# One-hot gathers on TensorE: the picks and sums of two units side by side, twice as many groups gathered wholly by TensorE, and the comparisons dealt out anew between VectorE and ScalarE

## The chip, the cores and the metric

The kernel runs on one core of a Trainium2 chip. A core has five engines that run at the same time, each through its own queue in order: TensorE (PE in the profile; its weight loads, PEld, are listed apart), VectorE (DVE), ScalarE (ACT), GpSimd (POOL) and SyncE (SP, which here only issues transfers). They wait for each other by semaphores. The metric is the device time of one execution in microseconds (us). The times before are the median of three runs; the profile is of one further execution.

## The reference

One layer of a graph network over 6250 nodes with 64 features and 206,250 edges, which are sorted by the node they point to (`dst`):

```python
h = jnp.maximum(_layernorm(x, axis=-1), 0.0)
msg = relu(h[src] + edge_attr)                      # one row per edge
agg = segment_sum(msg, dst, num_segments=6250)
x = x + relu((h + agg) @ W1 + b1) @ W2 + b2
```

The costly part is `h[src]`, a gather of 206,250 rows of 64 numbers, and the sum of the messages by `dst`.

## The kernel before

**Groups.** The edges are cut into 269 groups of 768: 128 partitions by 6 columns. The first five groups are a prologue, in which the layer norm is also made. For each later group GpSimd gathers three of the six columns, row by row, with indirect transfers (`gather`, L204, buffer `xg`), nine groups ahead. The other three columns are gathered by TensorE, as products with one-hot matrices. Three columns so treated are a *unit*. In 12 *whole* groups (`WHOLE`) TensorE gathers all six columns, and GpSimd none: such a group is two units. There are 276 units in 138 *sets* of two, and 46 *chunks* of three sets.

**How a row is picked.** A node's row of `h` lies in SBUF as three bf16 parts that add up to float32 (`hp`, 3x64 columns). The picking has two steps. In the first, the *slots*, `found` (a one-hot matrix: which node of 128 is wanted in each of 32 slots) multiplies `hp`: `slots_of`, L497, in column tiles of 128x32, 52 matmuls a unit. The result goes from PSUM (`half`, three banks in turn) to `picked` by a ScalarE copy (`slots_out`, L506). In the second step, the *picks*, `backs` (a one-hot matrix from slots to edges) multiplies `picked`: `pick`, L513, 18 matmuls of 128x128 weights a unit, 192 columns each. They add onto a PSUM bank that ScalarE has filled with the edge attributes (`room`, L522; two banks in turn). VectorE adds up the three parts (`messages`, L600), after it has added the gathered columns (L597), and ScalarE applies the relu (L602, `msg`).

**The one-hot matrices** are comparisons. `found` of a set has two blocks of 1536 columns and one of 256, for the last nodes (`find`, L465); all three are made by VectorE. `backs` of a set has six blocks of 768 columns: VectorE makes five (`back`, L484), and ScalarE the last in two passes, |a-b| and then relu(1-|a-b|) (`back_far` L474, `back_near` L477). What they compare against are lists of slots, broadcast to all partitions by SyncE's transfers (`source_load`, `spot_load`), one of each a set. The lists come from the *rank work* of a chunk: VectorE, TensorE and ScalarE find which slot each edge takes (`rank_at` to `source`, L280 to L347), about two chunks ahead; on TensorE these are the count (L285, L287), a transpose (L325) and the source matmuls (L339), all through one PSUM bank, `rows`.

**The sums.** For each unit a one-hot matrix of 32 nodes (`oh`, L581, two buffers) multiplies the messages: `window_sum`, L612, float32, column tiles of 128x64, 12 matmuls for six columns and 6 for three. The result lies in a corner of the first `half` bank. VectorE adds it to `z` two units later (`sum_into_z`, L575) at a column that it holds in a register; the columns of 16 groups are loaded into registers at a time (`window_start`, L442).

**Row blocks.** When all edges of 512 nodes are summed, the two dense layers follow: `hidden` (L631, TensorE, then ScalarE L634), `result` (L642, then L644) and `store` (VectorE L650 and L651, then a transfer), one step at each call of `blocks_behind`. There are 12 such blocks in the loop; `rows` serves them too.

**The order** is written out by hand, in `half(u)`, one call for each unit: what is called first is first in its engine's queue. For unit u of set k, TensorE gets: the sums of u-1, the slots of half of set k+1, the picks of u+1, the rank work if any. VectorE gets, in an even half: `messages(u)`, the one-hot of u, `backs` 3 and 4 of set k+1, z of u-2, row blocks, the first and the last block of `found` of set k+2. In an odd half: `messages(u)`, the one-hot, the second block of `found`, z of u-2, row blocks, `backs` 0 to 2 of set k+2. The rank work comes last in a half. The `beats` pace GpSimd's gathers: a gather waits for the TensorE instruction that its beat names.

Of the kernel before, what the change touches and what calls it, by code (L numbers as in the profile page):

```python
# [9 lines left out]
F32 = mybir.dt.float32  # L10
I32 = mybir.dt.int32
I16 = mybir.dt.int16
BF16 = mybir.dt.bfloat16
# [31 lines left out]
H = 3  # L45
# [13 lines left out]
F0 = 5  # L59
SETS = 3  # L60
RG = 2 * SETS
HEAD, PERIOD = 2 * RG - 1, 4 * RG - 1
assert (NG + 1 - F0 - HEAD) % PERIOD == 0
# [18 lines left out]
def kernel(  # L82
# [163 lines left out]

    def stretches(t_sb, c0, c1):

        n, g0 = (HEAD, F0) if c0 == 0 else (PERIOD, F0 + HEAD + (c0 - 2) // 4 * PERIOD)
# [201 lines left out]
    def source_load(k):  # L451
        sources[k] = rank.tile([P, PARTS * 2 * S], I16, name="sources")
        nc.sync.dma_start(out=sources[k][:PP], in_=lines[k // SETS][k % SETS].rearrange("(o m) s -> o (m s)", o=1)
                          .to_broadcast([PP, PARTS * 2 * S]))

    def spot_load(k):
        spots[k] = rank.tile([P, 2 * H * P], BF16, name="spots")
        nc.sync.dma_start(out=spots[k], in_=spot_rows[k * 2 * H:(k + 1) * 2 * H, :]
                          .rearrange("(o t) s -> o (t s)", o=1).to_broadcast([P, 2 * H * P]))

    def find(k, b):
# [3 lines left out]
        nc.vector.tensor_scalar(found[k][:, b * PARTS:b * PARTS + n].rearrange("p m i s -> p (m i s)"),  # L465
                                sources[k][:, :n * 2 * S], nodes_of[:, b:b + 1], None, op0=ALU.is_equal)

    far = const.tile([P, 1], F32, name="far")
    nc.vector.tensor_scalar_mul(far, ids[:, Q - 1:], -1.0)
    dists = {}  # L470

    def back_far(k):
        dists[k] = rank.tile([P, 2 * H * P], BF16, name="dist", bufs=1)
        nc.scalar.activation(dists[k], spots[k].bitcast(I16), AF.Abs, bias=far)  # L474

    def back_near(k):
        nc.scalar.activation(backs[k][:, Q - 1].rearrange("p t s -> p (t s)"), dists.pop(k), AF.Relu,  # L477
                             bias=ones[:, 0:1], scale=-1.0)

    def back(k, q0, q1):  # L480
        if q0 == 0:
            backs[k] = hot.tile([P, Q, 2 * H, P], BF16, name="backs")
        for q in range(q0, min(q1, Q - 1)):
            nc.vector.tensor_scalar(backs[k][:, q].rearrange("p t s -> p (t s)"), spots[k].bitcast(I16),  # L484
                                    ids[:, q:q + 1], None, op0=ALU.is_equal)
        if q1 == Q:
            spots.pop(k)
# [17 lines left out]
    def slots_out(k, n0):  # L505
        nc.scalar.copy(picked[k][:, n0:n0 + 2], halves.pop((k, n0)))  # L506
# [66 lines left out]
    def sum_into_z(u):  # L573
        at = window_start(group_of(u))
        nc.vector.tensor_tensor(z[:, ds(at, W)], z[:, ds(at, W)], aggs.pop(u), ALU.add)  # L575
# [96 lines left out]
    def is_set(k):  # L672
        return 0 <= k < KS

    def half(u):
        g = group_of(u)
        k, i = divmod(u, 2)
        first = ((0, 2), (6, 8))[i]
        later = ((4,), (10,))[i]
        now = is_set(k + 1)  # L680
        if is_first(u):
            enter(g + AHEAD, beats[-G + H:])
        if i == 0:
            if is_set(k + 3):
                source_load(k + 3)
        elif is_set(k + 3):
            spot_load(k + 3)
        window_sum(u - 1)
        if u + 1 < U:
            room(u + 1)  # L690
        if now:
            for n0 in first:
                begun = slots_of(k + 1, n0)
                slots_out(k + 1, n0)
                if n0 == first[0]:
                    beats.append(begun)
            for n0 in later:
                beats.append(slots_of(k + 1, n0))
        if u + 1 < U:
            beats.append(pick(u + 1, range(H)))  # L700
        messages(u)
        if now:
            for n0 in later:
                slots_out(k + 1, n0)
        one_hot(u)
        if i == 0:
# [17 lines left out]
        chunk(u + 13, rank_count)  # L724
        chunk(u + 12, rank_of)
        chunk(u + 11, rank_marks)
        chunk(u + 11, rank_turn)
        chunk(u + 10, rank_holds)
        chunk(u + 10, rank_fits)
        chunk(u + 9, source)  # L730
        if g in CHECKS and is_first(u):
            find_left(CHECKS.index(g))

# [59 lines left out]
    for g in range(F0):  # L793
        for i in range(g * LOOK // F0, (g + 1) * LOOK // F0):
            tails_begin(i)
        messages(g - F0)
        one_hot(g - F0)
        if g == 0:
            rank_at(1)
            rank_count(1)  # L800
        if g == 1:
            rank_of(1)
            rank_marks(1)
            rank_turn(1)
        if g == 2:
            rank_holds(1)
            rank_fits(1)
            source(1)
        if g == 3:
            rank_at(2)  # L810
            rank_count(2)
        if g >= 1:
# [10 lines left out]

    for b in range(BB + 1):
        find(0, b)
    back_far(0)
    back(0, 0, Q)
    back_near(0)
    for n0 in range(0, 2 * Q, 2):
        begun = slots_of(0, n0)  # L830
        slots_out(0, n0)
# [5 lines left out]
    beats.append(pick(0, range(H)))  # L837
    for b in range(BB + 1):
        find(1, b)
    back_far(1)  # L840
    back(1, 0, 3)
    for u in range(U):
        half(u)
# [84 lines left out]
```

## Time and profile before

| | |
|---|---|
| median of three runs | 1082.63 us (1082.12 to 1085.3) |
| the profiled execution | 1080.78 us, span 1079.1 us |
| TensorE's granted clock over the span | 0.974 of full |
| picks, L513 | 4968 matmuls |
| slots, L497 | 14352 matmuls |
| sums, L612 | 3224 matmuls |
| `backs` on VectorE, L484 | 690, busy 255.8 us |
| `found`, L465 | 414, busy 206.1 us |
| adding up the parts, L600 | 276, mean 749 ns |
| ScalarE's two passes for `backs`, L474 and L477 | 138 each, means 952 and 954 ns |
| ScalarE's copies to `picked`, L506 | 828, mean 480 ns |
| GpSimd's gathers, L204 | 754, mean 1007 ns |

In the profile's timeline a line has the start in us, the time from the first start to the last end in us, the engine, the line of the kernel, the operation, output and inputs with their shapes, and how many instructions were put together. In brackets stands how long the engine had been idle before it, and which instruction ended that. Starts on TensorE are measured; its matmuls overlap, so a start-to-start distance says more than a duration. VectorE's and ScalarE's instructions also overlap by some 0.08 us where they follow each other without a wait. In the answer for one line, "DVEq" is VectorE's sequencer; the three numbers are the least, the median and the greatest duration in ns. In the windows of the span the columns are the window, its length, the busy time of TensorE, its weight loads, VectorE, ScalarE and GpSimd with the number of instructions, the granted clock, the share of the DMA engines and GB/s.

### The profile page before, as it was taken

To read this page: it belongs to the slowest core of one execution; us is meant where nothing else is said; L and a number is where in the kernel's file an instruction comes from. 1 tells how busy PE (TensorE), PEld (TensorE's weight loads), DVE (VectorE), ACT (ScalarE), POOL (GpSimd) and SP (SyncE) were. 2 spreads that over 40 slices of the span, in tenths; PEclk is the share of its full clock that TensorE was granted. 3 is DMA by queue.
4 is the path that set the end of the run, shared out by engine and by line. 5 is a ranking of instruction groups with operands and counts; after the bars stand their busy time and mean duration, and the time that the engine had idled before them with its cause. 6 is when DMAs were issued, how large, how long until landed. Compare 5 with 4: busy or idle time off the path is not lost.

```text
span 1079.1 us, 55140 instructions
## 1 busy us (share of the span) xinstructions
PE 994.9 (92%) x23185; PEld 865.5 (80%) x23185; DVE 960.5 (89%) x2686; ACT 940.6 (87%) x1979; POOL 793.9 (74%) x798
## 2 busy tenths in 40 slices
PE   3159999999999999999999999999999999999997
PEld 2148888888878888888888888888888888888885
DVE  8869889898998998998999898998999898998984
ACT  6459889899989998898998998998998998998985
POOL 7677777777777777777777777777777777777740
PEclk9659999999999999999999999999999999999998
DMA  6445566565655665665665656565656665655650
GB/s 207 126 117 150 164 164 187 141 178 158 188 143 150 180 190 143 170 169 165 163 174 149 184 157 165 155 199 156 161 148 187 164 170 154 185 158 161 167 132 10
DMA packets 115098, 172.36 MB, mean 160 GB/s; under 512 B 28444, under 2 KB 83613, under 8 KB 114845
## 3 DMA queue, kind: packets, MB, share of 16 engines
q1 hardware_dynamic: 89752, 143.03, 43.7%
q0 software_dynamic: 25088, 25.74, 13.5%
q8 instruction: 184, 3.01, 1.1%
q14 instruction: 70, 0.57, 0.2%
q10 hardware_dynamic: 4, 0.01, 0.0%
HBM read 164.85 MB, written 3.84 MB: 156 GB/s over the span
## 4 chain that ended last, share of the span: by engine, by line
PE 76%; DVE 10%; issue 5%; DMA 4%; ACT 3%; POOL 1%; DVEq 1%; SPq 0%; ACTq 0%
PE pick L513 34%; PE half L497 26%; PE half L612 10%; DVE backs L484 2%; DVE found L465 2%; DVE ea L600 2%; DMA xg<-h_rows,src_sb 2%; PE rows L339 2%; PE rows L642 1%; PE rows L631 1%; PE rows L287 1%; POOL xr L204 1%; DMA x<-in_x_dram 1%; DVE oh L581 1%; PE rows L285 1%
## 5 line engine op out<-in xcount | busy, mean ns | idle before, releaser
L204 POOL DMA_INDIRECT xg<-h_rows,src_sb x754 | 759.4, 1007 | 231.6 <-issue 105.2
L513 PE MATMUL pick<-picked,backs 128*128 128x192 bf16 x4968 | 459.9, 247 | 1.1 <-ACT pick L522 1.1
L513 PEld LDWEIGHTS <-backs 128*128 128x128 bf16 x4968 | 397.5, 98 | 45.1 <-issue 43.6
L506 ACT CAST picked<-half 128x384 bf16<-128x384 f32 x828 | 370.4, 480 | 54.3 <-PE half L497 47.2
L497 PE MATMUL half<-hp,found 128*32 128x192 bf16 x14352 | 352.8, 248 | 7.5 <-DVE found L465 4.9
L497 PEld LDWEIGHTS <-found 128*32 128x32 bf16 x14352 | 286.6, 97 | 22.2 <-issue 5.1
L484 DVE TENSOR_SCALAR backs<-spots,ids 128x768 bf16<-128x768 int16 x690 | 255.8, 419 | 0.0
L600 DVE TENSOR_REDUCE ea<-pick 128x192 f32<-128x576 f32 x276 | 206.8, 749 | 21.6 <-PE pick L513 19.7
L465 DVE TENSOR_SCALAR found<-sources,nodes_of 128x1536 bf16<-128x1536 int16 (+1 forms) x414 | 206.1, 525 | 0.1
L612 PEld LDWEIGHTS half<-oh,msg 128*64 128x64 f32 x3224 | 121.7, 138 | 62.0 <-issue 27.4
L522 ACT COPY pick<-ea 128x576 f32<-128x576 f32 x264 | 170.4, 646 | 0.0
L612 PE MATMUL half<-oh,msg 128*64 128x32 f32 x3224 | 152.4, 227 | 13.5 <-DVE z L575 10.8
L602 ACT ACTIVATE msg<-ea 128x384 f32<-128x384 f32 (+2 forms) x281 | 146.3, 521 | 10.7 <-DVE ea L600 7.2
L477 ACT ACTIVATE backs<-dist,ones 128x768 bf16<-128x768 bf16 x138 | 131.7, 954 | 0.3 <-ACT dist L474 0.3
L474 ACT ACTIVATE dist<-spots,far 128x768 bf16<-128x768 int16 x138 | 131.4, 952 | 0.0
L575 DVE TENSOR_TENSOR z<-z,half 128x32 f32 x281 | 50.9, 181 | 73.2 <-ACT picked L506 43.5
L581 DVE TENSOR_TENSOR oh<-slot,slots 128x192 f32<-128x192 int16 (+2 forms) x281 | 94.5, 336 | 1.0 <-PE half L612 1.0
L597 DVE TENSOR_TENSOR ea<-ea,xg 128x192 f32<-128x192 f32 x252 | 87.4, 347 | 0.7 <-issue 0.7
L285 PE MATMUL rows<-at,upper 128*128 128x432 f16 x46 | 16.4, 358 | 21.7 <-DVE at L280 19.7
L339 PE MATMUL rows<-holds,marks 128*96 128x96 f16 x276 | 25.8, 231 | 11.4 <-DVE holds L313 5.0
L291 ACT CAST before<-rows 128x432 f16<-128x432 f32 x46 | 23.9, 519 | 14.3 <-PE rows L287 14.3
L344 ACT CAST source<-rows 24x64 int16<-24x64 f32 x138 | 28.1, 203 | 9.5 <-PE rows L339 4.4
(107 smaller groups left out, 435.1 us busy)
## 6 DMA issues: line engine op xcount, KB each, us to landing
sources<-source_row SPq DMA_DIRECT2D x138, 384.0 KB
ea<-in_edge_attr_dram SPq DMA_DIRECT2D x268, 192.0 KB
spots<-spot_rows SPq DMA_DIRECT2D x138, 192.0 KB
xg<-h_rows,src_sb POOLq DMA_INDIRECT x754
xb<-in_x_dram SPq DMA_DIRECT2D x12, 128.0 KB
out_dram<-o SPq DMA_DIRECT2D x12, 128.0 KB
h_rows<-x SPq DMA_DIRECT2D x3, 384.0 KB
dst_sb<-in_dst_main_dram SPq DMA_DIRECT2D x1, 804.0 KB
```

The costliest lines, as they stand in the source:

```text
L204: it = nc.gpsimd.indirect_dma_start(out=xg[:, j, :], out_offset=None, in_=rows[:, :], in_offset=bass.IndirectOffsetOnAxis(ap=idx[:, j:j + ...
L465: nc.vector.tensor_scalar(found[k][:, b * PARTS:b * PARTS + n].rearrange("p m i s -> p (m i s)"), sources[k][:, :n * 2 * S], nodes_of[:, b ...
L474: nc.scalar.activation(dists[k], spots[k].bitcast(I16), AF.Abs, bias=far)
L477: nc.scalar.activation(backs[k][:, Q - 1].rearrange("p t s -> p (t s)"), dists.pop(k), AF.Relu, bias=ones[:, 0:1], scale=-1.0)
L484: nc.vector.tensor_scalar(backs[k][:, q].rearrange("p t s -> p (t s)"), spots[k].bitcast(I16), ids[:, q:q + 1], None, op0=ALU.is_equal)
L497: last = nc.tensor.matmul(ps[j * S:(j + 1) * S, u], found[k][:, m, i, :], hp[:, min(m, RR - 1)].rearrange("p t d -> p (t d)"), start=(b == ...
L506: nc.scalar.copy(picked[k][:, n0:n0 + 2], halves.pop((k, n0)))
L513: last = nc.tensor.matmul(ps[:, u, :3].rearrange("p t d -> p (t d)"), backs[k][:, q, i * H + u, :], picked[k][:, i * Q + q], start=False, ...
L522: nc.scalar.copy(picks[u][:, :H, :3], parts)
L600: nc.vector.tensor_reduce(ea[:, c0:c0 + H], picks.pop(u)[:, :H, :3].rearrange("p j t d -> p j d t"), AX.X, ALU.add)
L602: nc.scalar.activation(msg[:, lo:hi], ea[:, lo:hi], AF.Relu)
L612: last = nc.tensor.matmul(pa[i * D:(i + 1) * D], msg[:, j, :], oh[:, j, :], start=(j < lo + 2), stop=(j >= hi - 2))
```

## The change

Four things are changed together.

1. The two units of a set are picked one behind the other. In an even half TensorE gets the sums of u-1, the first six slot columns of set k+1 and the picks of u+1; in an odd half the picks of u+1 first, then the last six slot columns, then the sums of u-1. So two units' picks, and two units' sums, are neighbours. ScalarE makes room for both banks in the even half.
2. Every eleventh group is whole, from the sixth of the loop on: 24 groups, not 12. There are 288 units, 144 sets and 48 chunks; GpSimd makes 718 gathers for the loop, not 754.
3. VectorE makes all six blocks of `backs`. ScalarE makes the small last block of `found`, in the same two passes.
4. On VectorE z of u-2 and z of u-1 both stand in the even half, with the row blocks behind each, and `backs` 3 to 5 of the next set behind them. The rank work starts one unit earlier, and one more of its steps stands in the prologue.

```diff
-HEAD, PERIOD = 2 * RG - 1, 4 * RG - 1
-WHOLE = [F0 + RG - 1] + list(range(F0 + HEAD + 2 * RG - 1, NG + 1, PERIOD))
+HEAD = PERIOD = 2 * RG - 1
+WHOLE = list(range(F0 + RG - 1, NG + 1, PERIOD))
...
     def find(k, b):
...
-        nc.vector.tensor_scalar(found[k][:, b * PARTS:b * PARTS + n].rearrange("p m i s -> p (m i s)"),
-                                sources[k][:, :n * 2 * S], nodes_of[:, b:b + 1], None, op0=ALU.is_equal)
...
+        to = found[k][:, b * PARTS:b * PARTS + n].rearrange("p m i s -> p (m i s)")
+        if b < BB:
+            nc.vector.tensor_scalar(to, sources[k][:, :n * 2 * S], nodes_of[:, b:b + 1], None, op0=ALU.is_equal)
+        else:
+            dist = rank.tile([P, J * 2 * S], BF16, name="dist", bufs=1)
+            nc.scalar.activation(dist, sources[k][:, :n * 2 * S], AF.Abs, bias=last_node)
+            nc.scalar.activation(to, dist, AF.Relu, bias=ones[:, 0:1], scale=-1.0)
...
     def back(k, q0, q1):
...
-        for q in range(q0, min(q1, Q - 1)):
+        for q in range(q0, q1):
...
+    def slots_by(k, n0s):
+        for n0 in n0s:
+            last = slots_of(k, n0)
+            slots_out(k, n0)
+            if n0 != n0s[1]:
+                beats.append(last)
...
     def half(u):
...
         if i == 0:
+            window_sum(u - 1)
             room(u + 1)
+            if is_set(k + 1):
+                slots_by(k + 1, (0, 2, 4))
             beats.append(pick(u + 1, range(H)))
+            messages(u)
+            if u + 2 < U:
+                room(u + 2)
+            one_hot(u)
+            for v in (u - 2, u - 1):
+                sum_into_z(v)
+                blocks_behind(v)
             if is_set(k + 1):
-                back_near(k + 1)
                 back(k + 1, 3, Q)
-            sum_into_z(u - LAG)
-            blocks_behind(u - LAG)
             if is_set(k + 2):
                 find(k + 2, 0)
                 find(k + 2, BB)
         else:
+            if u + 1 < U:
+                beats.append(pick(u + 1, range(H)))
+            messages(u)
+            if is_set(k + 1):
+                slots_by(k + 1, (6, 8, 10))
+            window_sum(u - 1)
+            one_hot(u)
             if is_set(k + 2):
-                back_far(k + 2)
-                find(k + 2, 1)
-            sum_into_z(u - LAG)
-            blocks_behind(u - LAG)
-            if is_set(k + 2):
                 back(k + 2, 0, 3)
+                find(k + 2, 1)
-        chunk(u + 14, rank_at)
+        chunk(u + 15, rank_at)
...
```

More of the change, by code (lines that the diff above doesn't have):

```diff
@@ L459, in spot_load @@
                           .rearrange("(o t) s -> o (t s)", o=1).to_broadcast([P, 2 * H * P]))
+    last_node = const.tile([P, 1], F32, name="last_node")
+    nc.vector.tensor_scalar_mul(last_node, nodes_of[:, BB:], -1.0)
     def find(k, b):
@@ L677, in half @@
         k, i = divmod(u, 2)
-        first = ((0, 2), (6, 8))[i]
-        later = ((4,), (10,))[i]
-        now = is_set(k + 1)
         if is_first(u):
             enter(g + AHEAD, beats[-G + H:])
-        if i == 0:
[L684 to L689, printed above, removed]
-            room(u + 1)
[L691 to L699, printed above, removed]
-            beats.append(pick(u + 1, range(H)))
[L701 to L706, printed above, removed]
+        if is_set(k + 3):
+            if i == 0:
+                source_load(k + 3)
+            else:
+                spot_load(k + 3)
+        if i == 0:
+            window_sum(u - 1)
+            room(u + 1)
+            if is_set(k + 1):
+                slots_by(k + 1, (0, 2, 4))
+            beats.append(pick(u + 1, range(H)))
+            messages(u)
[5 more added lines that the diff above has]
+                blocks_behind(v)
             if is_set(k + 1):
-                back_near(k + 1)
                 back(k + 1, 3, Q)
-            sum_into_z(u - LAG)
-            blocks_behind(u - LAG)
             if is_set(k + 2):
@@ L715, in half @@
         else:
[L716 to L720 removed]
+            if u + 1 < U:
[5 more added lines that the diff above has]
+            one_hot(u)
             if is_set(k + 2):
                 back(k + 2, 0, 3)
[L723 to L730 removed]
+                find(k + 2, 1)
+        chunk(u + 15, rank_at)
+        chunk(u + 14, rank_count)
+        chunk(u + 13, rank_of)
+        chunk(u + 12, rank_marks)
+        chunk(u + 12, rank_turn)
+        chunk(u + 11, rank_holds)
+        chunk(u + 11, rank_fits)
+        chunk(u + 10, source)
         if g in CHECKS and is_first(u):
```

18 lines of the change are left out of this document (4 added, 14 removed).

## The prediction

> **What bounds the kernel now.** I read the page first, then the chain, then the timeline of each engine, then the waits.
>
> ```profile
> PE 994.9 (92%) x23185; PEld 865.5 (80%) x23185; DVE 960.5 (89%) x2686; ACT 940.6 (87%) x1979; POOL 793.9 (74%) x798
> ...
> PE 76%; DVE 10%; issue 5%; DMA 4%; ACT 3%; POOL 1%; DVEq 1%; SPq 0%; ACTq 0%
> PE pick L513 34%; PE half L497 26%; PE half L612 10%; DVE backs L484 2%; DVE found L465 2%; DVE ea L600 2%; DMA xg<-h_rows,src_sb 2%; PE rows L339 2%; PE rows L642 1%; PE rows L631 1%; PE rows L287 1%; POOL xr L204 1%; DMA x<-in_x_dram 1%; DVE oh L581 1%; PE rows L285 1%
> ```
>
> TensorE is the chain: picks, slots and sums, in that order, in every unit. Its timeline over two units:
>
> ```profile
> 502.29 1.66 PE L513 MATMUL pick<-picked,backs 128*128 128x192 bf16 x18
> 503.79 0.56 PE L339 MATMUL rows<-holds,marks 128*96 128x96 f16 x6
> 504.27 0.54 PE L612 MATMUL half<-oh,msg 128*64 128x32 f32 x12
> 504.74 1.26 PE L497 MATMUL half<-hp,found 128*32 128x192 bf16 x52
> 505.93 1.66 PE L513 MATMUL pick<-picked,backs 128*128 128x192 bf16 x18
> 507.52 0.54 PE L612 MATMUL half<-oh,msg 128*64 128x32 f32 x12
> ```
>
> Starts count here, the ends are modelled. Sums to slots 0.47 us, slots to picks 1.19, picks to sums 1.59: a unit is 3.25 us with no gap. A stage that is followed by another width of weights pays for the switch: picks followed by the 96-column source matmuls take 1.50 us (503.79-502.29, 0.083 each), by the 64-column sums 1.59, so 0.09. Slots are 13 rounds of four at 0.083, 1.07 us, so 0.12 of their 1.19 is switch; sums stream in 0.35 and switch in 0.12. 276 units fill 897 us of the span. Between 80 and 1060 us I find only 21.4 us in which TensorE starts late against these spacings (the two waits of a row block, below, apart), 12.8 of them at one event, VectorE's register load.
>
> VectorE is close behind:
>
> ```profile
> 502.12 0.34 DVE L581 TENSOR_TENSOR oh<-slot,slots 128x192 f32<-128x192 int16 x1
> 502.39 0.60 DVE L465 TENSOR_SCALAR found<-sources,nodes_of 128x1536 bf16<-128x1536 int16 x1
> 502.92 0.17 DVE L575 TENSOR_TENSOR z<-z,half 128x32 f32 x1
> 503.01 1.06 DVE L484 TENSOR_SCALAR backs<-spots,ids 128x768 bf16<-128x768 int16 x3
> 504.00 0.34 DVE L597 TENSOR_TENSOR ea<-ea,xg 128x192 f32<-128x192 f32 x1
> 504.27 0.74 DVE L600 TENSOR_REDUCE ea<-pick 128x192 f32<-128x576 f32 x1
> 504.94 0.34 DVE L581 TENSOR_TENSOR oh<-slot,slots 128x192 f32<-128x192 int16 x1
> ```
>
> Start to start: one-hot 0.27, found 0.53, z 0.10, backs 0.33 each, add 0.27, reduce 0.67. Every 16 groups it also loads 16 node numbers into registers:
>
> ```profile
> L442 DVEq TENSOR_LOAD <-dst_sb x17: 2945/3604/3847, 58.9 to 1028.7; - x17
> ```
>
> ```profile
> 189.50 0.61 DVE L465 TENSOR_SCALAR found<-sources,nodes_of 128x1536 bf16<-128x1536 int16 x1
> 192.22 0.19 DVE L575 TENSOR_TENSOR z<-z,half 128x32 f32 x1 [2.11 <-ACT pick L522]
> ```
>
> ```profile
> 192.56 0.54 PE L612 MATMUL half<-oh,msg 128*64 128x32 f32 x12 [1.16 <-DVE z L575]
> ```
>
> The load at 188.43 (3.60 us, on the sequencer) ran ahead of three queued instructions; the z behind it came 0.19 us after its end, VectorE stood idle 2.1 us and TensorE 1.2. Sixteen such loads fall into the loop, at 0.8 us of TensorE each.
>
> **The change, part by part.** The sum is made against the profiled execution: 1080.78 us, span 1079.1, and 1.7 around it; the median of the three runs is 1.85 above it.
>
> *Twelve more units, paired.* Call the two units of a set e and e+1, and the set's two halves by them. TensorE's order in a set becomes sums, sums, slots, picks A, rank work, picks B, slots (the later six columns). Streams 2x(0.35+1.07+1.49)=5.82, switches 0.12 and 0.12 as now, picks to slots and slots to sums new: 0.10 and 0.11 taken, 6.27 in all against 6.50. The nearest rows are 0.09 (picks to sums) and 0.12 (slots to picks); from 0 to 0.12 for each: -30 to +4 us over 144 sets. 144x6.27=902.9 against 276x3.25=897.0; the sums of a whole group's unit are 0.12 shorter (0.35 from start to slots at 427.43): 48 such units against 24. **+3.0**. The four switches a set, for six, pay for the six sets more.
>
> *Rank work* stands after picks A in each set. Count costs 0.43 there (0.58 from 510.68 to the sums, less the switch), source 0.41, the transpose 0.25, now between two 128-wide stages and so with two switches. 48x1.09 against 46x1.03: **+4.9**.
>
> *Row blocks.* The hidden product, its result and the rank work share one PSUM bank, so a follower waits for ScalarE's copy:
>
> ```profile
> 153.80 1.07 PE L631 MATMUL rows<-z,w_sb 128*64 128x512 f32 x2
> 155.64 0.56 PE L339 MATMUL rows<-holds,marks 128*96 128x96 f16 x6 [0.77 <-ACT h L634]
> ```
>
> 1.84 us where rank work follows, about 0.83 net where sums follow; a result 1.56 (0.83 and a wait of 0.73) against 1.03. Before, 6 and 5 of 12 met rank work. In the changed program all 12 blocks come due at u-2 of one kind of half, so hidden, result and count follow each other: 12x3.5=42 against 32. **+10**.
>
> *ScalarE* drops two passes of 0.95 us per set for two over 256 elements (0.3 to 0.5 by the 192- and 384-wide rows). It was not what ends the waits for long, so nothing is gained but slack. In the new order it must make room for picks B: copies at 1.47, 1.84, 2.21 us of the set, msg 2.58, room 3.00 to 3.65; picks B start at 3.75 or later. And the first sums of the next set need the copy of slots 6: ready 6.27+r, wanted 6.28+r, where r is the rank work. Both are just in time; 0 taken, up to 0.1 a set, 14 us.
>
> *VectorE* gets the sixth backs (+0.33) and loses the small found (-0.2): a set is 2 z 0.31, 6 backs 1.98, 2 found 1.06, 2 adds 0.54, 2 reduces 1.34, 2 one-hots 0.54, 5.77 us, and rank work of 0.93, 0.37 and 1.17 in the three sets: 6.70, 6.14, 6.94, against TensorE's 6.53, 6.69, 6.71. That is 99%, 98% with whole groups. It falls behind by at most 0.40 before the middle set returns it. What it may fall behind follows from the set, counted from the first sums: slots at 0.82; the first copy at 1.47 (0.65 later, as 532.59 and 533.24 show), done 1.95; z of u-2, which waits for that copy, at 1.98; second z 2.19; the last three backs at 2.29, 2.62, 2.95, done 3.37. Picks B begin at 3.50+r and load the sixth weights at 3.81+r, 4.06 to 4.24. Spare: 0.65 to 0.83 us. So ordinary sets run without waits, and the 21.4 us go: **-21.4** (0 to -21.4).
>
> *The register loads* now stand before one of those z, and the backs that picks B need at once are queued behind it. In the built order the one-hot of half e waits for the sums of e-2 (0.6 us), and the sequencer stops there, so the load runs from 0.6 to 0.95 and z comes at 4.4 to 4.75 instead of 1.98: 2.4 to 2.8 late, less the spare 1.65 to 2.1. That holds where the group's first unit is even, 8 of 16: 15.2 us. Where it is odd the load stands between the two z, behind the wait for the copy: from 2.0 to 5.6, second z at 5.8 instead of 2.19, picks B 2.8 to 2.95 late: 8, 23.0 us. **+38.2**; between 0.8 each (before) and the load's 3.6: 13 to 58. I take the layout, since each step has its row. The lag left over costs about 0.4 in the count and transpose sets: **+4** (0 to 14).
>
> *The clock.* After TensorE's longest wait in the loop it ran at half speed for 3.4 us:
>
> ```profile
> 1050.32 0.19 PE L423 MATMUL rows<-ones,most 128*1 128x1 f32 x2 [1.97 <-DVE most L421]
> ```
>
> ```profile
> 1051.00:1055.00 4.00, 4.00 (x68) 3.60 (x69) 3.59 (x11) 2.89 (x6) 0.00 (x0) 0.58 0.02 4
> ```
>
> That is 1.7 us lost; waits of 1.5 us and less left the clock at 1.00. The odd loads make a pause of 2.2 us, the same; half of them taken: **+6.8** (0 to 27 for all sixteen). [...]
>
> *Nothing for* 36 gathers fewer (they land 24 to 33 us before their add) and the loads on SP's queue, 12 more broadcasts at a DMA share of 0.6, each issued a set before use; if that cover went, VectorE's first backs or found would wait. Start +0.4: six backs for five before the first picks.
>
> Sum: 3.0+4.9+10-21.4+38.2+4+6.8+0.4=+45.9: **1127 us**, 4% slower.
>
> **The rivals.**
> 1. *Loads hidden*: VectorE runs a set ahead, so that the late z meets no one. Then 1080.8+17.9-21.4+0.4=1078: not slower. It decides at about 0.3 us a load. For it: run-ahead of up to seven instructions in the trace. Against: z waits for this set's copy, so no lead can build. 0.08.
> 2. *Loads as dear as before*, 0.8: 1127-25-4-7=1091. For it: before, VectorE's idle 2 us cost TensorE 0.8. Against: there the backs were wanted a set later. 0.08.
> 3. *New switches free*, since narrow weights go in beside the picks: 1097. Against: picks to the 18-column transpose pay 0.09 too. 0.08.
> 4. *VectorE the bound*: its set runs 0.4 us longer, for the many waits in its queue; it has 0.17 to spare, so 144x0.23=33 more, 1160. Against: z to z is the only new wait. 0.08.
> 5. *Clock at every load*, at 1.7 us: 1127-6.8+27=1147. Against: half the pauses are shorter than the one that cost clock. 0.08.
> 6. *Clock never falls*: the pause is cut up by three picks before and single picks within, unlike the one at 1050.32: 1120. 0.18. [...]
>
> **Numbers.** Forecast 0.42. 1090 to 1148 leaves out rivals 1 and 4. Within 0.3%, about what a measurement of this kernel tells from no change, lies half of rival 1: faster 0.04, same 0.04, slower 0.92.
>
> **What would show it.** Starts of two picks groups 1.49 us apart plus rank work; slots 52 to sums 1.17 to 1.19; TensorE busy evenly with sixteen gaps of 1.7 to 2.9 us inside picks after a load, released by backs; VectorE idle 2.3 or 3.5 us before a z at each; ScalarE's share near 72% (940.6 less 138x1.9, plus 144x0.7 and twelve units at 2.2). Wrong if gaps appear in every set (VectorE or ScalarE late), or none at the loads.

## The result and the profile after

| | before | changed |
|---|---|---|
| median, us | 1083.97 (4 runs) | 1148.2 (1144.75 to 1150.18, 4 runs) |
| ratio, with its 95% interval | | 1.0587 (1.0551 to 1.0624) |
| profiled execution, us | 1080.78 | 1148.84 |
| its span, us | 1079.1 | 1147.1 |

The change makes the kernel 5.9% slower. The sign is the predicted one; the sum gave 1127, and 1148.2 lies 0.2 us above the upper end of the range. The kernel before took 1083.97 us this time; set against the 1082.63 us that the forecast knew, the ratio gives 1146.

The page of the changed kernel, engine shares and granted clock by fortieths of the span:

```profile
PE 1034.1 (90%) x24045; PEld 902.5 (79%) x24045; DVE 1009.0 (88%) x2784; ACT 875.8 (76%) x2073; POOL 765.9 (67%) x762
...
PEclk9569999999989999999999998999999998999998
```

ScalarE fell from 87% to 76% and TensorE, with 860 matmuls more, from 92% to 90%: something makes it wait. The chain of this profile breaks off after 2% of the span, so it can't say what; the timelines do. TensorE over two sets without a load:

```profile
535.70 1.26 PE L493 MATMUL half<-hp,found 128*32 128x192 bf16 x52
536.93 0.89 PE L608 MATMUL half<-oh,msg 128*64 128x32 f32 x24
537.75 1.26 PE L493 MATMUL half<-hp,found 128*32 128x192 bf16 x52
538.94 1.66 PE L509 MATMUL pick<-picked,backs 128*128 128x192 bf16 x18
540.43 0.35 PE L285 MATMUL rows<-at,upper 128*128 128x432 f16 x1
...
540.90 1.67 PE L509 MATMUL pick<-picked,backs 128*128 128x192 bf16 x18
542.50 1.26 PE L493 MATMUL half<-hp,found 128*32 128x192 bf16 x52
543.74 0.77 PE L608 MATMUL half<-oh,msg 128*64 128x32 f32 x18
```

This is the predicted set: two units' sums together, slots 0.82 us after them, picks A 1.19 later, the rank work, picks B, slots. From the sums at 536.93 to those at 543.74 it takes 6.81 us. By kind of rank work the median distance of two sums groups is 6.76 for a set with a count and 24 sums, 6.54 for one with a source and 18, 6.42 for one with a transpose and 18; the prediction's set gives 6.70, 6.56 and 6.40. So where nothing waits, the pairing costs what was reckoned, but for 0.06 in each count. Sets with a transpose and 24 sums are the exception: the reckoning gives 6.52, and the median of the 19 that ran at full clock is 6.86. The difference is a wait between slots and sums, 0.33 us in the median, of which more below.

What waits is seen behind a register load. VectorE and TensorE at the load that begins at 252.0 (one timeline; in brackets the idle time before an instruction and what ended it):

```profile
253.23 0.42 PE L509 MATMUL pick<-picked,backs 128*128 128x192 bf16 x3
...
256.04 0.19 DVE L571 TENSOR_TENSOR z<-z,half 128x32 f32 x1 [3.60 <-issue]
256.15 1.07 DVE L480 TENSOR_SCALAR backs<-spots,ids 128x768 bf16<-128x768 int16 x3
256.61 0.10 PEld L509 LDWEIGHTS <-backs 128*128 128x128 bf16 x1 [3.19 <-DVE backs L480]
256.62 2.92 PE L509 MATMUL pick<-picked,backs 128*128 128x192 bf16 x15 [2.96 <-DVE backs L480]
```

TensorE does three picks of B, then stands, because VectorE's queue is z (late by the whole load), then the three backs that the fourth pick needs. The 15 picks that follow take 2.92 us instead of 1.4, for a second reason that comes below: half clock. The chain of cause that the prediction described, load, z, backs, picks B, is there in its order, with its names. The loads themselves are the old ones (operation and count; shortest, median and longest, ns):

```profile
L442 DVEq TENSOR_LOAD <-dst_sb x17: 2942/3603/3846, 59.1 to 1096.3; - x17
```

The waits by line, in all of the span (total us, times, longest us):

```profile
PEld L509 <- DVE backs L480: 35.7, 48, 3.2
...
PEld half L608 <- ACT picked L502: 31.3, 134, 2.2
DVE z L571 <- PE rows L627: 27.7, 11, 3.9
...
PE pick L509 <- DVE backs L480: 24.6, 15, 3.0
```

Fifteen long waits of picks for backs are the loads. The two other lines were not in the sum: sums that wait for ScalarE's copy of the slots, and a z that waits for the hidden product of a row block. The latter keeps VectorE idle for 27.7 us in 11 blocks. At the block that begins at 155.65, whose lines are shown further down, that z came 2.41 us late, and the picks at 159.52 ran through all the same, since the block's own steps held TensorE for longer. In the seven sets with a block that ran at full clock, picks waited 0.1 us together.

I measured TensorE's start-to-start distances between 76 us and 15 us before the end against their spacings without a wait, and split what is over into waits and into the loss at half clock:

| us | before | changed | difference | forecast |
|---|---|---|---|---|
| streams (12 units, switches, rank work, blocks without their waits) | | | +11.6 | +9.4 |
| waits of the row blocks | 10.3 | 17.8 | +7.5 | +8.5 |
| picks waiting for backs | 2.8 | 37.7 | | +42.2 (loads 38.2, lag 4) |
| all other waits | 19.8 | 15.7 | with the 2.8 above: 22.6 before, 15.7 now | -21.4, none new |
| half clock | 2.5 | 20.6 | +18.1 | +6.8 |
| start | | | | +0.4 |
| span | 1079.1 | 1147.1 | +68.0 | +45.9 |

The streams' +11.6 are what is left of the span's +68.0 when the other rows are taken off; the forecast's +10 for the row blocks stands here as 8.5 of waits and 1.5 of stream. Against the forecast the span came out 22.1 us longer: 11.3 for the clock and 15.7 for waits where none were reckoned, less 4.9 for the other rows together. Of the 15.7, 9.8 stand between slots and sums. Not all of the rest is new: the one wait for `most` near the end is 2.7 us, and was 2.0 before.

### The profile page after: what moved, and what is told of

Read it like the earlier page. It is cut to its first block, busy times and chain, and to the rows that moved or that the text cites. A ratio compares the mean times of both kernels' runs of the same rounds, so it can differ in the third digit from the quotient of the medians.

```text
span 1147.1 us, 56664 instructions
## 1 busy us (share of the span) xinstructions
PE 1034.1 (90%) x24045; PEld 902.5 (79%) x24045; DVE 1009.0 (88%) x2784; ACT 875.8 (76%) x2073; POOL 765.9 (67%) x762
## 5 line engine op out<-in xcount | busy, mean ns | idle before, releaser
L204 POOL DMA_INDIRECT xg<-h_rows,src_sb x718 | 731.3, 1018 | 321.5 <-PE half L493 100.6
L509 PE MATMUL pick<-picked,backs 128*128 128x192 bf16 x5184 | 499.1, 250 | 28.8 <-DVE backs L480 24.6
L509 PEld LDWEIGHTS <-backs 128*128 128x128 bf16 x5184 | 430.5, 100 | 70.7 <-DVE backs L480 35.7
L502 ACT CAST picked<-half 128x384 bf16<-128x384 f32 x864 | 359.9, 485 | 95.1 <-PE half L493 81.9
L493 PEld LDWEIGHTS <-found 128*32 128x32 bf16 x14976 | 302.4, 98 | 39.4 <-issue 26.7
L480 DVE TENSOR_SCALAR backs<-spots,ids 128x768 bf16<-128x768 int16 x864 | 316.2, 419 | 0.0
L598 ACT ACTIVATE msg<-ea 128x384 f32<-128x384 f32 (+1 forms) x293 | 148.5, 507 | 104.2 <-DVE ea L596 99.8
L470 DVE TENSOR_SCALAR found<-sources,nodes_of 128x1536 bf16<-128x1536 int16 x288 | 177.0, 615 | 0.0
L608 PEld LDWEIGHTS half<-oh,msg 128*64 128x64 f32 x3224 | 111.1, 140 | 36.1 <-ACT picked L502 31.3
L608 PE MATMUL half<-oh,msg 128*64 128x32 f32 x3224 | 128.1, 227 | 9.5 <-ACT picked L502 6.6
L577 DVE TENSOR_TENSOR oh<-slot,slots 128x192 f32<-128x192 int16 (+1 forms) x293 | 95.9, 327 | 5.8 <-PE half L608 5.7
L474 ACT ACTIVATE found<-dist,ones 128x256 bf16<-128x256 bf16 x144 | 73.2, 508 | 5.4 <-ACT dist L473 0.7
L473 ACT ACTIVATE dist<-sources,last_node 128x256 bf16<-128x256 int16 x144 | 74.5, 517 | 0.0
```

The costliest lines, as they stand in the source:

```text
L204: it = nc.gpsimd.indirect_dma_start(out=xg[:, j, :], out_offset=None, in_=rows[:, :], in_offset=bass.IndirectOffsetOnAxis(ap=idx[:, j:j + ...
L470: nc.vector.tensor_scalar(to, sources[k][:, :n * 2 * S], nodes_of[:, b:b + 1], None, op0=ALU.is_equal)
L493: last = nc.tensor.matmul(ps[j * S:(j + 1) * S, u], found[k][:, m, i, :], hp[:, min(m, RR - 1)].rearrange("p t d -> p (t d)"), start=(b == ...
L509: last = nc.tensor.matmul(ps[:, u, :3].rearrange("p t d -> p (t d)"), backs[k][:, q, i * H + u, :], picked[k][:, i * Q + q], start=False, ...
L577: nc.vector.tensor_tensor(oh[:, lo:hi], slot[:, g * G + lo:g * G + hi].unsqueeze(2).to_broadcast([P, n, W]), slots.unsqueeze(1).to_broadca ...
L598: nc.scalar.activation(msg[:, lo:hi], ea[:, lo:hi], AF.Relu)
```

## The experiments

Runs told of together under one heading were on one chip and share the runs of the kernel before, where nothing else is said; ratios are to those.

### The parts alone

The kernel before took 1080.35 us (7 runs). Four kernels take the change apart.

**The changed kernel with small loads.** Eight loads of two numbers in place of one of sixteen:

```diff
-RV = 16
+RV = 2
```

> The changed kernel with register loads of 2 node numbers instead of 16 (16 take 3.60 us and 13 take 2.95, so some 0.22 each: 2 take about 0.5 us, eight times as often). Theory 'the load is what delays': a load of 0.5 us hides in the spare of 0.65 to 0.83 us before picks B, so the waits inside picks fall from 37.7 us to under 5, the clock stays at full in the loop (20.6 us back), and most of the sums' waits (9.8 us) go: 1148 - 33 - 20 - 6, about 1089 us. Rival 'VectorE is the bound': its sequencer spends as long on loads in all (144 loads of 0.5 us), so the waits only spread out: above 1130 us.

Measured 1110.09 us, 1.0259 (1.0226 to 1.0292): 38 us less than the changed kernel (whose kernel before ran at 1083.97), but 21 more than the theory's 1089, and not the rival's 1130. The load itself shrank as wanted:

```profile
L442 DVEq TENSOR_LOAD <-dst_sb x135: 326/512/756, 59.4 to 1104.3; - x135
```

Waits inside picks fall from 37.7 to 9.8 us. What remains is in other places: 17 us at row blocks, 12.4 between slots and sums (70 times), 12.8 us of half clock. The second of these is seen in the set before the sums at 252.19, in the timeline of this run:

```profile
250.46 0.75 DVE L596 TENSOR_REDUCE ea<-pick 128x192 f32<-128x576 f32 x1
...
251.24 0.52 ACT L598 ACTIVATE msg<-ea 128x384 f32<-128x384 f32 x1 [1.75 <-DVE ea L596]
...
251.67 1.22 ACT L502 CAST picked<-half 128x384 bf16<-128x384 f32 x3
252.18 0.78 PEld L608 LDWEIGHTS half<-oh,msg 128*64 128x64 f32 x24 [0.55 <-ACT picked L502]
252.19 0.89 PE L608 MATMUL half<-oh,msg 128*64 128x32 f32 x24 [0.32 <-ACT picked L502]
```

ScalarE stood idle for 1.75 us, in front of the second unit's message, whose reduce VectorE had not made. The copy of slots 6 is behind that message on ScalarE's queue, and the first sums of the next pair need the bank that it frees. So VectorE's lateness reaches TensorE on a second path, through an engine that is 76% busy.

**The kernel before with small loads.** The same edit there:

> The kernel before with loads of 2 numbers. Theory: the sixteen loads cost it 12.8 us of waits and hardly any clock, so 1084 - 12 = 1072 us. If loads were as dear before as after: 1084 - 50 = 1034 us.

Measured 1065.22 us, 0.986 (0.9825 to 0.9896). The expected 1072 was reckoned from 1084; beside its own kernel before the run is 15 us shorter, where 12 were expected, so the loads were not as dear there as in the changed kernel. Of the 15 us 12.8 were seen as TensorE's waits.

**The kernel before with 24 whole groups.** Order and comparisons as before, only the pattern of groups changed (the slices of the edge numbers follow it):

```diff
-HEAD, PERIOD = 2 * RG - 1, 4 * RG - 1
-WHOLE = [F0 + RG - 1] + list(range(F0 + HEAD + 2 * RG - 1, NG + 1, PERIOD))
+HEAD = PERIOD = 2 * RG - 1
+WHOLE = list(range(F0 + RG - 1, NG + 1, PERIOD))
```

> The kernel before with the 24 whole groups and nothing else of the change: 12 units more at 3.25 us, less 12 x 0.12 us of shorter sums, and two chunks of rank work at 1.03: +39.6 us, 1124 us, if TensorE is the bound and GpSimd's 36 gathers fewer are worth nothing. Rival: if GpSimd had been the bound before, the units would come cheaper: under 1100 us.

Measured 1126.44 us, 1.0417 (1.0377 to 1.0458). Twelve groups moved from GpSimd to TensorE cost 46 us, where 39.6 were expected: 3.8 for each added unit, where a unit without a wait is 3.25. That GpSimd had been the bound is out, since the units didn't come cheaper.

**The changed order and comparisons with 12 whole groups.** The opposite edit in the changed kernel.

> The changed order and the changed comparisons with the 12 whole groups of before (276 units). Theory 'TensorE pays by the unit': 6 sets fewer at 6.27 us, two chunks fewer at 1.09, sums 1.4 longer: -38 us, 1110 us, waits at the loads as in the changed kernel. Rival 'GpSimd sets the pace once units are shorter' (754 gathers at 1.26 us are 948 us, from 50 us on): no lower than about 1140 us, with VectorE's adds waiting for gathers.

Measured 1111.03 us, 1.0273 (1.0243 to 1.0304), the theory's 1110 and not the rival's 1140: 31 us for the pairing with its new comparisons. Waits inside picks are 42.3 us and half clock 25.0, somewhat more than in the full change (37.7 and 20.6). So the loads' cost belongs to the pairing, with the comparisons and the VectorE order that came with it, and not to the added units; which of these three it is, only the run with the backs first, below, begins to tell. 1.0417 times 1.0273 is 1.070 against 1.0587: a further unit is cheaper in the paired order (37 us for twelve, 1148 less 1111, taken over two chips whose kernels before differ by 3.6 us).

### The same kernels on slower chips

The next four, and two more later, were run on two other chips, where the kernels that ran on both kinds of chip took 28 to 34% longer: the kernel before 1428.43 us (7 runs) in the first set and 1452.99 us (14 runs) in the second. There TensorE stands still without waiting for anything that the profile shows, in a way that hides what was to be measured. PE and PEld in after_blocks, in the second set ("issue" is such a wait):

```profile
PE half L493 <- issue: 83.1, 197, 0.5
```

```profile
PEld L493 <- issue: 169.7, 424, 0.8
PEld L509 <- issue: 139.8, 284, 1.4
```

The changed kernel on its own chip has 0.9 us in 2 waits, 26.7 in 150 and 25.5 in 154 on these three. VectorE's `backs` there take 426 ns each against 419, and GpSimd's gathers 1019 against 1018, so these two engines run nearly as ever. The granted clock of their profiled runs, 0.955 to 0.965, is that of the changed kernel (0.960), so it isn't the clock. With some 330 to 390 us of TensorE's waits in each of these six runs, ratios shrink towards 1, and expectations in microseconds that rest on 1080 can't be held against these runs. Why TensorE's instructions start late there, and whether it lies in the chip, stays open.

**The later backs ahead of the z.** In the changed kernel, `back(k + 1, 3, Q)` goes out ahead of the two `sum_into_z`:

```diff
             one_hot(u)
+            if is_set(k + 1):
+                back(k + 1, 3, Q)
             for v in (u - 2, u - 1):
                 sum_into_z(v)
                 blocks_behind(v)
-            if is_set(k + 1):
-                back(k + 1, 3, Q)
```

> The changed kernel with the last three backs ahead of the two z on VectorE, loads of 16 as they are. Theory 'the backs queued behind the late z are what TensorE waits for, and the lateness then comes out one step later': the waits inside picks go (37.7 us to under 5), but z, the next found and the reduce of e+1 are as late as before, ScalarE's msg with them, and the copy of slots 6 that the sums wait for stands behind that msg: the waits between slots and sums rise from 9.8 us to 30 to 40, and the time stays within 1148 +- 12 us. Rival 'only the backs matter': 37.7 us of waits and the clock's 20 go, about 1090 us.

1439.1 us, 1.0073 (1.0057 to 1.009): it was run once more, below.

**Loads of eight numbers.** `RV = 8` in the changed kernel.

> The changed kernel with loads of 8 numbers: 1.84 us each by 0.22 a number, 33 of them. Layout: z late by 0.7 to 1.0 us where the group's first unit is even, which the spare of 0.65 to 0.83 covers but for 0.2; where it is odd 1.84 late, 1.1 of wait: 16 x 0.2 + 16 x 1.1 = 21 us of waits inside picks, sums' waits as with loads of 2 (12.4). Theory 'the clock falls after a pause of some 2 us': none of these pauses reaches that, so the clock's loss is that of loads of 2 (12.8 us, after row blocks): 1110 + 12 = 1122 us. Rival 'every load costs clock': 33 dips, 1160 us.

1444.04 us (2 runs), 1.011 (1.0089 to 1.013). Waits inside picks are 13.5 us there, against 37.7 with sixteen on the other chip, but the time can't be compared.

**A combination: small loads, 12 whole groups, row blocks at one place.** The changed order with `RV = 2` and the old pattern of groups, and the row blocks asked for once a set, in the odd half between the second unit's picks and the last six slot columns, in place of behind each z (the lines for the groups are left out here):

```diff
             for v in (u - 2, u - 1):
                 sum_into_z(v)
-                blocks_behind(v)
...
             messages(u)
+            blocks_behind((u - 3, u - 2))
             if is_set(k + 1):
                 slots_by(k + 1, (6, 8, 10))
```

> The changed order and comparisons with 12 whole groups, loads of 2, and one step of a row block a set, in the odd half between picks and slots, where no rank work follows. Theory: from 1110 (24 groups, loads of 2) 38 us for the units, 17 us of waits for ScalarE's copies in the shared PSUM bank, less 5, and some 10 us of clock that follow those waits: about 1050 us, below both kernels. Rival 'GpSimd sets the pace' (754 gathers of 1.26 us from 50 us on end at 1000 at the earliest): gathers late and over 1070 us.

1420.18 us, 0.9929 (0.9905 to 0.9954); run once more, below.

**The combination with the copy first.** On top of it, slots 6 and their copy go out ahead of the second unit's message. The row blocks' step moves as well, from ahead of the slots to behind them, so two things differ:

```diff
+            if is_set(k + 1):
+                last = slots_of(k + 1, 6)
+                slots_out(k + 1, 6)
+                beats.append(last)
             messages(u)
-            blocks_behind((u - 3, u - 2))
             if is_set(k + 1):
-                slots_by(k + 1, (6, 8, 10))
+                last = slots_of(k + 1, 8)
...
+            blocks_behind((u - 3, u - 2))
             window_sum(u - 1)
```

> The same, with the copy of slots 6 ahead of msg on ScalarE, and the row blocks' step behind the slots. Theory 'the sums wait for that copy, which stands behind msg, which waits for VectorE': the waits between slots and sums (12.4 us with loads of 2) go to under 3, some 8 us below pairs12_rv2_blocks. Rival: the sums of e+1 then wait for msg instead, and nothing is won.

1421.4 us, 0.9948 (0.9931 to 0.9965).

**The copy first once more, and the blocks alone.** In the second set pairs12_copy_first was run again, and the row blocks moved to that one place alone, in the changed kernel:

> The changed kernel, its loads of 16 numbers kept, with the row blocks asked for at one place behind both halves of a set instead of behind each z. Theory (the two waits of a block, 10.3 and 6.7 us in all, stand one behind the other with only a result between them, and bring half clock for 3.4 us behind some of the twelve): both waits go, and with them five or so of the fourteen half-clock stretches at 1.7 us: 1148 less 17 less 4 to 9, 1122 to 1127. Rival (the clock falls for the register loads alone, and VectorE, which is short of time, turns what TensorE saves into other waits): the waits behind slots grow by as much as the blocks' shrink, the clock loss stays at 20 us, and the time stays above 1140.

1451.22 us (10 runs), 0.999 (0.9973 to 1.0007). The waits of the blocks (10.3 and 6.7 us) are no longer in the trace, which the theory asked for; whether the time goes with them isn't told by such a chip. Half-clock loss is 23.1 us, but on such a chip the pauses without a shown cause may make it too, so the second half of the question stays open.

> pairs12_rv2_blocks with ScalarE's copy of slots 6 ahead of the second unit's message, so that the first sums of the next pair no longer wait for VectorE's reduce by way of that copy. A repeat of pairs12_copy_first, whose chip ran the kernel before at 1428 us. Theory (that copy is what ends the 24.7 us of waits between slots and sums in pairs12_rv2_blocks_b): most of them go, and the time falls from 1066 to 1042 to 1050, below the kernel before with small loads. Rival (VectorE, 92% busy, is late by itself, and its reduce then holds up the message, which the same sums need): the waits between slots and sums stay above 15 us, and the time stays at 1058 to 1068.

1442.59 us, 0.9936 (0.9914 to 0.9958). On the first such chip this kernel and the one without its edit were alike (0.9948 and 0.9929, intervals that meet). Nor do the waits fall there: sums that wait for ScalarE's copies (PE half L608 <- ACT picked L502) make 12.5 us in 47 waits without the edit, 13.6 in 51 and 12.6 in 48 with it. That the copy's place is worth anything was not shown.

### Backs first, and the combination, on a chip like the first

Here the kernel before took 1082.05 us (7 runs).

> The changed kernel with its loads of 16 numbers, and the three later backs written out ahead of the two z. A repeat of after_backs_first, whose chip ran the kernel before at 1428 us. Theory (the late z holds up the backs that picks B need, and nothing else makes the loads dear): picks after a load no longer wait for backs, the waits inside picks fall from 38 us to under 10, and the time goes from 1148 to 1110 to 1120. Rival (VectorE simply has no time for the 3.6 us of a load, so that the wait moves to the sums, through the z and the accumulators that sums wait for): waits of 1.5 us or more appear behind the picks at every load instead, and the time stays at 1140 to 1155.

Measured 1124.56 us (1121.69 to 1124.94), 1.0383 (1.0359 to 1.0407): 24 us less than the changed kernel, 4.6 short of the theory's nearest figure, and far from the rival's. The rival's mechanism is there all the same, at a smaller price. The load that begins at 183.1:

```profile
184.84 1.66 PE L509 MATMUL pick<-picked,backs 128*128 128x192 bf16 x18
...
186.88 0.19 DVE L571 TENSOR_TENSOR z<-z,half 128x32 f32 x1 [3.06 <-issue]
186.98 0.61 DVE L470 TENSOR_SCALAR found<-sources,nodes_of 128x1536 bf16<-128x1536 int16 x1
187.12 1.26 PE L493 MATMUL half<-hp,found 128*32 128x192 bf16 x52 [0.62 <-DVE z L571]
```

All 18 picks run through; the slots behind them now wait 0.62 us for the late z, which frees their bank, and at the end of these slots the sums wait another 1.57. Waits inside picks are 3.8 us in all (37.7), between picks and slots 6.0 (none), between slots and sums 20.7 (9.8). At the sixteen loads together the waits are 21 us instead of 33. So the queue place of the backs decided about a third of what a load costs in waits; the rest is VectorE's missing 3.6 us, which come out one or two stages later.

> The changed order and comparisons with 12 whole groups, register loads of two numbers, and the row blocks asked for at one place behind both halves of a set. A repeat of pairs12_rv2_blocks, whose chip ran the kernel before at 1428 us. On a chip that runs the kernel before at about 1080 us: after_12 (1111) less what the small loads gave the changed kernel (38 us) gives 1073, less some 4 us if the two waits of a block no longer come one behind the other: 1069, so within 5 us of before_rv2's 1065. Theory: the pairing itself brings nothing beyond the four switches for six, since each unit takes TensorE 3.1 us either way. Rival: the pairing is worth the 15 us that its switches count (0.12 a switch, one a unit saved), and the time is 1050 or less.

Measured 1065.88 us (1064.41 to 1067.66), 0.9845 (0.9824 to 0.9865): the theory's 1069 and 1065, not the rival's 1050. The blocks' waits are gone, since the hidden product and the result now have other work behind them:

```profile
232.20 1.07 PE L627 MATMUL rows<-z,w_sb 128*64 128x512 f32 x2
233.21 1.26 PE L493 MATMUL half<-hp,found 128*32 128x192 bf16 x52
```

Only 1.6 us are lost at half clock (after_12: 25.0). But the reason that the expectation gave does not stand. Against before_rv2 this kernel's TensorE waits 46.3 us instead of 19.8, of which 24.7 between slots and sums (85 times), and its profiled span is 2.2 us longer (1066.0 and 1063.8), with the same clock loss. So its streams are 24 us shorter: the four switches for six bring most of what they count (138 sets at 6.50 less 6.27 are 32 us, less 3 for the rank work's added switches), and the waits of the paired order take it all back. The waits' row for it, which names ScalarE's copy:

```profile
PEld half L608 <- ACT picked L502: 43.1, 118, 2.3
```

This kernel and before_rv2 are the two fastest, 1.4 to 1.6% below the kernel before, and their intervals overlap.

## Why the prediction was right or wrong

**Direction, and the main term: right.** *The register loads* were put at +38.2, with 1.65 to 2.1 us where the group's first unit is even and 2.8 to 2.95 where it is odd. From the changed kernel's picks: the eight even loads cost 1.36 to 2.16 us, 1.67 in the mean; seven odd ones cost 2.21 to 3.63, 2.76 in the mean, and the eighth nothing, since the waits of a row block lay over it. Together 32.6 us (13.3 and 19.3), and 5.1 in all other picks, for *the lag*'s +4. Small loads take some 36 us out of the time (1.0587 less 1.0259, of 1084), 28 of them in the waits of picks and 8 in clock. That rivals 1 and 2 are out follows from this: a load costs 2.0 us of waits alone, not 0.3 or 0.8.

**Units, switches and rank work: right.** 11.6 against 9.4, with 0.06 more in each of 48 counts. Rival 3, switches that are free, is out by the sets' lengths.

**Row blocks: right in size,** 7.5 against 8.5 of waits: the eleven blocks of that stretch all met a result and then a count, 11 times 0.94 and 11 times 0.61:

```profile
155.65 1.07 PE L627 MATMUL rows<-z,w_sb 128*64 128x512 f32 x2
157.49 1.10 PE L638 MATMUL rows<-w_sb,h 64*128 64x64 f32 x8 [0.77 <-ACT h L630]
159.06 0.34 PE L285 MATMUL rows<-at,upper 128*128 128x432 f16 x1 [0.46 <-ACT o L640]
```

**"Ordinary sets run without waits, and the 21.4 us go": half right.** Before, such waits came to 22.6 us; in the changed kernel they come to 15.7, and 9.8 of these stand in a place where there were none. The step that failed is the ScalarE one: "the copy of slots 6: ready 6.27+r, wanted 6.28+r ... Both are just in time; 0 taken, up to 0.1 a set, 14 us". 9.8 us were measured there, in 52 sets; in sets with a transpose and 24 sums it was 0.33 in the median. The bound held and the value taken, nothing, did not. The working had looked at VectorE's spare on one path alone, by z and backs to picks B (0.65 to 0.83 us). The other path, reduce, message, copy of slots 6, first sums, has hardly any, and VectorE, reckoned at 98 to 99% of a set, is late on it whenever something stands in front of the reduce: the marks of a transpose set (0.36 us in the built order), a row block's two additions (0.87 us).

**"Half of the odd loads" cost clock, +6.8: the mechanism was there, the size was not.** 18.1 us more are lost. What decides isn't the length of a pause alone. In the changed kernel's trace, in its record of the clock, all half-speed stretches in the loop are 3.413 us long or a whole multiple of it, and they begin on one fixed grid: from 255.88 to 334.39 are 23 such steps, to 341.21 another 2, to 392.41 another 15. Cut along that grid, the profile shows when it falls (length and busy time of PE, PEld, DVE, ACT, POOL, granted clock, DMA share, GB/s):

```profile
252.47:255.88 3.41, 1.18 (x13) 0.73 (x10) 0.00 (x0) 1.76 (x5) 2.74 (x3) 1.00 0.36 82
255.88:259.29 3.41, 2.67 (x15) 2.00 (x15) 3.25 (x10) 0.21 (x1) 0.00 (x0) 0.50 0.28 88
...
450.44:453.85 3.41, 1.37 (x14) 0.98 (x11) 0.65 (x3) 2.17 (x6) 2.63 (x3) 1.00 0.78 224
...
187.61:191.03 3.42, 1.91 (x27) 1.43 (x31) 2.65 (x8) 0.00 (x0) 0.94 (x1) 1.00 0.35 92
184.20:187.61 3.41, 2.56 (x46) 1.95 (x34) 0.19 (x1) 2.98 (x8) 2.68 (x3) 1.00 0.43 104
```

The wait of 2.24 us at 451.6 lies almost wholly in one window, TensorE is busy for 1.37 of it, and the next window runs at half speed. The wait of 2.39 us at 186.5 is longer, but the grid cuts it at 187.61; the halves are busy for 2.56 and 1.91 us, and the clock stays. Seven windows of the changed kernel in which TensorE was busy for 1.18 to 1.78 us were each followed by a half-speed one, and the one with 1.91 was not. Between 1.8 and 2.3 us busy time as the profile models it doesn't decide: four windows with row blocks had 2.18 to 2.20 and were followed by a half-speed one, three others with 2.12 to 2.17 were not. So windows in which TensorE was busy for 35 to 52% of the time (1.18 to 1.78 of 3.41 us) were enough.

So five of the eight odd loads paid, one of them for two windows, and one even load: seven windows for the four of the forecast. The second window of the one came behind a first, the half-speed one from 255.88, of which TensorE filled 2.67 us; the twelve other half-speed windows of the loop in this trace, with 3.22 us or more busy, were followed by full speed. Four row blocks paid too, whose two waits of 0.94 and 0.61 with half-empty stages between them fall into one window, and one wait of 1.9 us in front of the sums at 332.64. These five windows were not in the term at all; in the run with small loads, blocks are most of what is left of it, and with blocks and loads both disarmed 1.6 us remain. *Rival 5*, clock at every load, gives 1147 by its sum, close to the time measured, but not by its mechanism: ten of sixteen loads cost no clock. *Rival 6*, no clock, is out.

**Rival 4, VectorE the bound,** at 33 us for a lag in every set, was the nearest in spirit to what was missed: VectorE is late, in a third of the sets and by 0.2 us, through ScalarE's queue. Its reason for being unlikely, that z to z is the only new wait, was wrong: in a row block z also waits for the hidden product.

**ScalarE's share** came to 76%, not 72: its two passes over 256 elements took 0.52 and 0.51 us each, where 0.3 to 0.5 were reckoned.

## What to carry to other kernels

When a schedule is tightened until an engine has, by its forecast, 2% to spare, follow each of its products to its reader, and through the queue of every engine in between: the spare is that of the shortest path, and an engine at 76% can hand on another's lateness. A long instruction on the sequencer of such an engine, here one load of sixteen register values, is better cut into small ones: that alone made the old kernel 1.4% faster and the new one 3.3 points less slow. Before a pause is priced at its length, see how much work it leaves TensorE in a clock window (in the changed kernel's trace the eight windows with 1.8 us or less of 3.4 each cost the next one); two short waits near each other did that there, the row blocks' 0.94 and 0.61 us, as one long one did.

## What the runs showed of the hardware

- In the changed kernel's trace all half-speed stretches of the loop begin on a fixed grid of 3.413 us. They came behind all eight windows of it in which TensorE was busy for 1.8 us or less (0.88 to 1.79), and behind none with 2.3 or more at full clock; in the kernel before behind the one with 1.44, and behind none with 2.0 or more. A wait of 2.24 us cost 1.7 us more, one of 2.39 nothing: the grid left 1.37 us of work in one window of the first, 2.56 and 1.91 in the two of the second. Between 1.8 and 2.3 the bound isn't told: in the changed kernel four windows with row blocks had 2.18 to 2.20 us and were followed by a half one, five others with 1.91 to 2.27 were not, and the ends of matmuls are modelled.
- In the same trace the half-speed window with 2.67 us of TensorE busy was followed by another, the twelve with 3.22 or more by full speed.
- VectorE's register loads took 3.60 us for sixteen numbers and 2.94 for thirteen in the changed kernel, and 0.51 for two in the same with small loads, about 0.22 us a number. What stood behind a load on VectorE's queue waited for all of it (at the load of 252.0 in the changed kernel VectorE was idle for 3.60 us); what was queued ahead of it ran on meanwhile (at the load of 188.43 in the kernel before, VectorE was idle for 2.1 of the 3.6 us).
- One and the same program took 1080 to 1084 us on some occasions and 1428 to 1453 us on two others, each on another chip, with TensorE waiting for nothing that the profile shows. Ratios between kernels from such a run, 1.0073 where the other gave 1.0383 for the same kernel, don't carry over.
